# A two-layer graph attention network: W1's product by Strassen's half products, and x brought back in layer 2 by an identity product

## The chip, the core and the metric

The kernel runs on one core of one Trainium2 chip, in one launch. Each number called a time is the device time of one execution in microseconds. TensorE is called PE, VectorE DVE, ScalarE ACT, GpSimd POOL and SyncE SP, as the profile calls them.

## The reference

There are N = 10000 nodes with 768 numbers each and 170000 edges, sorted by destination, self loops among them; the network adds one more self loop per node. The reference computes

```python
h  = gat(x, W1, a_src1, a_dst1, b1)          # 768 -> 4 heads x 256
h1 = relu(layer_norm(h, g1, be1)) + x @ Wr1 + br1
h  = gat(h1, W2, a_src2, a_dst2, b2)         # 1024 -> 1 head x 768
h2 = layer_norm(h, g2, be2) + h1 @ Wr2 + br2
out = layer_norm(x + h2)                     # all in fp32
```

where `gat` multiplies by W, takes a softmax over the edges of each destination of `leaky_relu(alpha_src[src] + alpha_dst[dst])`, and sums the sources' rows with these weights.

## The kernel before

The nodes are handled in 79 tiles of 128 (NT = 79). The kernel has three parts, one after the other, and in each the order of instructions is written out by hand: an engine takes its instructions in the order in which the Python code issues them, and there is no planner.

**The projection** makes `x @ W1` for one tile after the other. `product` (its matmul is L172) issues six contraction steps for each of two halves of 512 columns into one PSUM tile of two banks called `big`. An fp32 matmul shows as two records in the trace. ACT copies the product to `row` (L667). DVE multiplies the product, read from PSUM, by `ad_b` and `as_b` (L670), and ACT sums each head's 256 elements (L673): these are the nodes' parts of the logits. POOL adds `b1` to `row` (L675), and SP stores the row to `table1`. After each tile one step is taken from a list of steps, which consists of two generators that run side by side:

- `prepare` sorts the edges into slots: for 80 columns it counts how many entries of `most` (128x1408) lie below an id, three counts a step, all on DVE (L240 into `less`, then the cast L242 to `at`, gathers of edge chunks by POOL at L245, and the remainder L231, L233). Later come the prefix sums over degrees (L277 adds into `before`), ranks, 79 scatters on POOL (L314), and the windows of sources that become `slots`.
- `weight_steps` multiplies W2 with the attention vectors (L645, L646), and computes two products with br1, the bias of the first residual, since the residual is kept without it: `after2`, which is `be2 + br2 + br1 @ Wr2` made in eight pieces (L653, added at L654), and `shift` and `lift`, which are `br1 @ W2`.

**Layer 1** gathers neighbours. POOL issues one indirect DMA for each slot (L425: 128 rows of 1033 floats from `table1`) into a ring of slots in SBUF, in the order of tiles; a gather waits until the slot's old row has been read. Nodes are sorted by degree into tiles, and the tiles' slots rise and then fall over the layer, 1377 in all; the ring holds 29 of them in layer 1 and 41 in layer 2. For a tile the logits (L478) need all its rows. The weighted sum is split: a few slots on PE as products with diagonal matrices, which ACT makes from `ident` (`summed`: L735 makes a `[P, H1, P]` buffer per slot, of which there are three, and L739 multiplies), the others on DVE (L520, or L516 after ACT's L509). `from_x` transposes the tile's gathered rows of x on PE for the residual product with Wr1 (L709), then POOL adds `after2` to the same rows (L717) and SP stores them to `x_d`. `L573` to `L589` are the layer norm (statistics, Ln and Exp on ACT, scaling), `L809` adds the residual, and L826 multiplies the result with W2.

**Layer 2** gathers rows of `table2` in the same way. Per tile PE makes the residual `h1 @ Wr2` (`residual`, L946, into `big`), and into free columns of the same PSUM tile the last 256 columns of the weighted sum (L934, with diagonals by ACT at L933, and a bias product L929); DVE sums the first 512 columns (L520). `norms` finishes a tile: statistics L573, then `scaled` (L587, L589) with g2 as factor and, in place of be2, the row `x + after2` that layer 1 stored, so that x, br2 and br1's part come in as the first norm's bias. Then

```python
nc.vector.scalar_tensor_tensor(h, r[:, :C2], 1.0, h, op0=OP.mult, op1=OP.add, accum_out=total)   # L957
```

adds the residual and sums it, and six small and two wide ACT instructions (L961 to L966, with a Square over 768 elements at L962 for the variance) make the last norm. `fetch_x` loads h1 and `x_d` for the tile after next by SP, `x_d` into one of three buffers (`xs`).

Of the kernel before, what the change touches and what calls it, by code (L numbers as in the profile page):

```python
# [28 lines left out]
F32 = mybir.dt.float32  # L29
# [6 lines left out]
P = 128  # L36
# [43 lines left out]
def gnn_kernel(ctx, tc, x, x_cols, src, dst, src_col, dst_col, W1, a_src1, a_dst1, b1, g1, be1, Wr1, br1,  # L80
# [57 lines left out]
    after2 = consts.tile([P, C2], F32, name="after2")  # L138
# [52 lines left out]
    def prepare():  # L191

        with tc.tile_pool(name="prep", bufs=1, side="right") as pool, \
                tc.tile_pool(name="prep2", bufs=2, side="right") as pool2:
            rows = pool.tile([P, NA, P], I32, name="rows")
            nc.sync.dma_start(rows, bass.AP(tensor=dst.tensor, offset=0, ap=[[P, P], [P * P, NA], [1, P]]))
            nxt = pool.tile([P, NA, P], I32, name="nxt")
# [7 lines left out]
            fall = pool2.tile([P, NA * P], F32, name="less", bufs=1).rearrange("p (a e) -> p a e", e=P)  # L205
# [9 lines left out]
            for a in range(NA):  # L215
# [6 lines left out]
                           allow_small_or_imprecise_dtypes=True)  # L222
            whole = pool.tile([P, NB], F32, name="whole")
# [12 lines left out]
            for j in range(0, NB, STEP):  # L236
                m = min(STEP, NB - j)
                for i in range(j, j + m):
                    less = pool2.tile([P, NA * P], F32, name="less", bufs=1)
                    nc.vector.tensor_scalar(less, most.rearrange("p a e -> p (a e)"), ids[:, i:i + 1], 0.0,  # L240
                                            op0=OP.is_lt, op1=OP.add, accum_out=whole[:, i:i + 1])
                nc.vector.tensor_copy(at[:, j:j + m], whole[:, j:j + m])  # L242
                chunk = pool2.tile([P, STEP, P], I32, name="chunk")
                for i in range(m):
                    nc.gpsimd.indirect_dma_start(  # L245
                        out=chunk[:, i, :], out_offset=None, in_=dst.rearrange("(c e) o -> c (e o)", e=P),
                        in_offset=bass.IndirectOffsetOnAxis(ap=at[:, j + i:j + i + 1], axis=0))
                for r in asked:
                    remainder(*r)
                asked = [(j, m, chunk)]  # L250
                yield
# [22 lines left out]
            before = pool.tile([P, NT + 1, D], BF16, name="before")  # L274
# [12 lines left out]
            facts = pool.tile([P, NT, 4], I32, name="facts")  # L287
# [11 lines left out]
            while s < D:  # L299
                more = pool.tile([P, D], F32, name=f"more{s}")  # L300
                nc.vector.tensor_add(more[:, :D - s], base[:, :D - s], base[:, s:])
                nc.vector.tensor_copy(more[:, D - s:], base[:, D - s:])
                base, s = more, 2 * s
# [38 lines left out]
            others = [pool.tile([P, NT, 4], I32, name=n) for n in ("rows", "nxt", "info")]  # L342
# [260 lines left out]
    with tc.tile_pool(name="w1", bufs=1) as w1p, tc.tile_pool(name="l1", bufs=2) as io, \  # L603
            psum_for_products(), tc.manual_schedule():
# [23 lines left out]
        def weight_steps():  # L628

            with nc.allow_non_contiguous_dma(reason="1024 numbers"):
                nc.scalar.dma_start(br1_c, br1.rearrange("(k p) -> p k", p=P))
            yield
            yield
            brT = spread_br1(w1p, "brT")
            load(w2, W2)
            nc.sync.dma_start(after2, bass.AP(tensor=be2.tensor, offset=be2.offset, ap=[[0, P], [1, C2]]))
            part = spread(w1p, br2, "part", nc.sync)
            for i, a in enumerate((a_dst2, a_src2)):  # L640
                vec = spread(w1p, a, "a2")
                for k in range(K1):
                    yield
                    m = io.tile([P, C1], F32, name="scr")[:, :C2]
                    nc.vector.tensor_mul(m, w2[:, k, :C2], vec)  # L645
                    nc.scalar.activation(m, m, AF.Copy, accum_out=w2[:, k, C2 + i:C2 + i + 1])  # L646
            load(wr1, Wr1)
            nc.vector.tensor_add(after2, after2, part)
            for k in range(K1):
                part = w1p.tile([P, C2], F32, name="part")  # L650
                nc.sync.dma_start(part, Wr2[k * P:(k + 1) * P, :])
                yield
                q = product(brT[:, k:k + 1, :], part[:, None, :], C2)  # L653
                nc.vector.tensor_add(after2, after2, q[:, :C2])  # L654
            yield
            q = product(brT, w2, R2)
            row = io.tile([P, R1], F32, name="row")
            nc.scalar.copy(row[:, :R2], q[:, :R2])
            nc.vector.tensor_add(lift, row[:, C2:C2 + 1], row[:, C2 + 1:R2])
            nc.scalar.dma_start(shift, row[0:1, :C2])  # L660
# [3 lines left out]
        for t in range(NT):  # L664
            p = product(xTs.pop(t), w1, C1)
            row = io.tile([P, R1], F32, name="row")
            nc.scalar.copy(row[:, :C1], p[:, :C1])  # L667
            for i, vec in enumerate((ad_b, as_b)):
                m = io.tile([P, C1], F32, name="scr")
                nc.vector.tensor_mul(m, p[:, :C1], vec)  # L670
                for h in range(H1):
                    s = slice(h * DH1, (h + 1) * DH1)
                    nc.scalar.activation(m[:, s], m[:, s], AF.Copy,  # L673
                                         accum_out=row[:, C1 + i * H1 + h:C1 + i * H1 + h + 1])
            nc.gpsimd.tensor_add(row[:, :C1], row[:, :C1], b1_b)  # L675
            load_x(t + 2)
            nc.sync.dma_start(table1[t * P:(t + 1) * P, :R1 - 1], row[:, :R1 - 1])
            next(steps, None)
# [9 lines left out]
    def ordered_layer1():  # L688
        nc.scalar.add_instruction(mybir.InstLoadActFuncSet(name=nc.get_next_instruction_name(), act_func_set_id=6, engine=nc.scalar.engine))
        with tc.tile_pool(name="b1", bufs=1) as pool, tc.tile_pool(name="small1", bufs=2) as small, \  # L690
# [22 lines left out]
            def from_x(t):  # L713

                xT = pool.tile([P, K0, P], F32, name="xT")
                moves = halves(xT, xt)
                nc.gpsimd.tensor_add(xt, xt, after2)  # L717
                nc.sync.dma_start(x_d[t], xt)
                return xT, moves
# [10 lines left out]
            def summed(acc, e, q, lo, hi, m):  # L730

                for k in range(lo, hi):
                    diagonals = pool.tile([P, H1, P], F32, name="diagonals", bufs=3)
                    for i in range(H1):
                        nc.scalar.activation(diagonals[:, i, :], ident, AF.Copy, scale=e[:, k, i:i + 1])  # L735
                    for i in range(H1):

                        c, d = i * DH1, (i + 1) * DH1
                        nc.tensor.matmul(acc[:, c:d], diagonals[:, i, :], ring.slot(q + k)[:, c:d],  # L739
# [4 lines left out]
            def weights_of(t):  # L744
# [5 lines left out]
                acc = ps_acc.tile([P, 2 * BANK], F32, name="acc")  # L750
                for lo, hi in ((0, min(m, 2)), (min(m, 2), m)):
                    summed(acc, e, FIRST[t], lo, hi, m)
                    yield acc
# [23 lines left out]
            for t in range(NT + 1):  # L777
# [66 lines left out]
                if live and not whole:  # L844
# [5 lines left out]
                    def some(q, e):  # L850
                        m = min(ON_PE1, e.shape[1])
                        summed(sums, e, q, 0, m, m)
                        return sums, m
# [22 lines left out]
    def ordered_layer2():  # L876
        nonlocal ps_big
        with tc.tile_pool(name="b2", bufs=1) as pool, tc.tile_pool(name="small2", bufs=2) as small, \
# [15 lines left out]
            firsts = [at_end(C1) for _ in range(min(2, NT))][::-1]  # L894
            xs = [parts[2][:, :D0], parts[3][:, :D0], after2]

            def fetch_x(t):

                hT = firsts[t] if t < 2 else parts[t % 2]
                nc.sync.dma_start(hT, h1_d[t])  # L900
                nc.sync.dma_start(xs[t % 3], x_d[t])
                return hT.rearrange("p (k n) -> p k n", n=P)
# [3 lines left out]
            added = spread(pool, shift, "out", nc.sync)  # L906
            b2_b = spread(pool, b2, "b2", nc.sync)
            ins[1] = fetch_x(1)
            g2_b = spread(pool, g2, "g2", nc.sync)
            nc.vector.tensor_add(b2_b, b2_b, added[:, :C2])  # L910
# [27 lines left out]
            def residual(t):  # L938


                hT = ins.pop(t)
                r = ps_big.tile([P, 2 * BANK], F32, name="big")
                for c in range(0, C2, BANK):
                    d = min(C2, c + BANK)
                    for j in range(K1):
                        nc.tensor.matmul(r[:, c:d], hT[:, j, :], wr2[:, j, c:d], start=(j == 0),  # L946
# [4 lines left out]
            def norms(t, h, r, means):  # L951
# [3 lines left out]
                scaled(h, means, stats, g2_b, xs[t % 3])  # L955
                total = small.tile([P, 1], F32, name="all")
                nc.vector.scalar_tensor_tensor(h, r[:, :C2], 1.0, h, op0=OP.mult, op1=OP.add, accum_out=total)  # L957
                yield
                o = pool.tile([P, C2], F32, name="out")
                less = small.tile([P, 1], F32, name="less")  # L960
                nc.scalar.activation(less, total, AF.Copy, scale=-1.0 / C2)  # L961
                nc.scalar.activation(o, h, AF.Square, bias=less, accum_out=total)  # L962
                nc.scalar.activation(total, total, AF.Ln, bias=eps, scale=1.0 / C2)
                nc.scalar.activation(total, total, AF.Exp, scale=-0.5)
                nc.scalar.activation(less, less, AF.Copy, scale=total)
                nc.scalar.activation(o, h, AF.Identity, bias=less, scale=total)  # L966
# [5 lines left out]
            assert C2 % BANK and C2 % BANK + C2 - ON_PE2 <= BANK  # L972
            rs = {0: residual(0)}
# [3 lines left out]
            for t in range(NT):  # L977
# [11 lines left out]
                else:  # L989
# [21 lines left out]
                    for _ in last:  # L1011
                        pass
                    last = norms(t, h, rs[t], [acc, rs[t][:, C2:2 * C2 - ON_PE2]])
# [274 lines left out]
```

## The time and the profile before

| | |
|---|---|
| runs | 5824.71, 5810.66, 5822.92 us |
| median | 5822.92 us |
| profiled execution | 5824.71 us, span 5822.9 us, mean granted PE clock 0.907 |
| busy share of the span | PE 84%, DVE 72%, POOL 57%, ACT 50% |
| DMA | mean 274 GB/s, 1594 MB moved, 1287 MB of it by POOL's queue |
| stages (read from the first and last instructions of each) | projection to 935 us, layer 1 to 3705 us, layer 2 to the end |

The busy share is a mean over three stages that have different limits, so each stage is read by itself. "Idle before" in a group of instructions is the time in which the engine stood still just ahead of them, with the instruction that ended most of that. A number behind an x is a count of instructions.

### The profile page before, as it was taken

Reading aid. Unit: us, or ns where it says so; the run is one execution under the profiler, and the core shown is the slowest. Engines: PE = TensorE matmul, PEld = TensorE weight load, DVE = VectorE, ACT = ScalarE, POOL = GpSimd, SP = SyncE. Lnnn points to the kernel's source line nnn. Section 1 sums busy time; section 2 is a strip of 40 time slices with the busy share of each in tenths; the row PEclk is TensorE's granted clock in tenths of the full one; section 3 lists DMA queues with packets and bytes.
Section 4 is the critical chain, followed back from the end, with each engine's and each line's share of the span. In section 5 each row is a group of like instructions: output and inputs, shape, how many; then the busy total and the mean of one; then the engine's idle time right before and its main releaser. Section 6 shows DMA issues by size and latency. Waiting matters only on the chain. (4 is left out here: it accounts for less than half of the span.)

```text
span 5822.9 us, 58833 instructions
## 1 busy us (share of the span) xinstructions
PE 4867.7 (84%) x14875; PEld 2883.8 (50%) x14875; DVE 4202.1 (72%) x7498; ACT 2927.9 (50%) x8500; POOL 3346.5 (57%) x3238
## 2 busy tenths in 40 slices
PE   9899996999988766568888999798888756778898
PEld 3344443555555444344555555455555534455565
DVE  5765244998877776778778899587766756767787
ACT  3333443777766665667766777343333323333333
POOL 3435465666555655655556665366666656666664
PEclk9999998999999888788999999899888877888899
DMA  4323636898888875778888898699998878889896
GB/s 156 122 93 84 89 93 228 312 344 333 306 309 317 323 291 215 286 294 306 317 316 334 335 341 302 245 334 329 328 314 301 311 255 291 305 309 318 313 339 216
DMA packets 475455, 1594.46 MB, mean 274 GB/s; under 512 B 118456, under 2 KB 122616, under 8 KB 475111
## 3 DMA queue, kind: packets, MB, share of 16 engines
q0 software_dynamic: 322384, 1286.62, 60.9%
q1 hardware_dynamic: 150672, 300.58, 15.5%
q10 hardware_dynamic: 2054, 3.42, 0.2%
q8 instruction: 125, 2.05, 0.1%
q14 instruction: 220, 1.79, 0.1%
HBM read 1434.95 MB, written 177.29 MB: 277 GB/s over the span
## 5 line engine op out<-in xcount | busy, mean ns | idle before, releaser
L425 POOL DMA_INDIRECT ring<-table,slots x2675 | 2619.6, 979 | 1353.4 <-issue 664.0
L520 DVE SCALAR_TENSOR_TENSOR acc<-ring,e,acc 128x512 f32<-128x512 f32 (+1 forms) x2530 | 1582.1, 625 | 219.2 <-PE acc L739 117.7
L509 ACT ACTIVATE ring<-ring,e 128x256 f32<-128x256 f32 x3284 | 1339.1, 506 | 12.9 <-issue 12.2
L516 DVE TENSOR_TENSOR acc<-acc,ring 128x1024 f32<-128x1024 f32 x801 | 985.6, 1230 | 82.0 <-issue 6.7
L934 PE MATMUL big<-ring,diagonals 128*128 128x256 f32 x2754 | 762.1, 433 | 274.9 <-issue 202.5
L946 PE MATMUL big<-wr,w 128*128 128x512 f32 (+1 forms) x2464 | 862.9, 503 | 110.9 <-issue 109.4
L172 PE MATMUL big<-w,xT 128*128 128x512 f32 x1896 | 834.4, 601 | 41.1 <-issue 18.5
L739 PE MATMUL acc<-ring,diagonals 128*128 128x256 f32 x1912 | 536.8, 441 | 376.4 <-ACT diagonals L735 203.8
L172 PE MATMUL big<-wr,xT 128*128 128x512 f32 x1896 | 835.2, 597 | 0.2 <-issue 0.2
L826 PE MATMUL half<-w,hT 128*128 128x512 f32 (+1 forms) x2528 | 830.4, 486 | 0.0
L934 PEld LDWEIGHTS big<-ring,diagonals 128*128 128x128 f32 x2754 | 594.0, 219 | 444.8 <-issue 281.9
L946 PEld LDWEIGHTS big<-wr,w 128*128 128x128 f32 x2464 | 483.4, 197 | 473.8 <-issue 441.1
L933 ACT ACTIVATE diagonals<-ident,e 128x128 f32<-128x128 f32 x1377 | 422.5, 388 | 550.6 <-remote 256.5
L739 PEld LDWEIGHTS acc<-ring,diagonals 128*128 128x128 f32 x1912 | 425.3, 225 | 479.7 <-ACT diagonals L735 220.7
L826 PEld LDWEIGHTS half<-w,hT 128*128 128x128 f32 x2528 | 477.8, 189 | 372.8 <-issue 327.4
L172 PEld LDWEIGHTS big<-w,xT 128*128 128x128 f32 x1896 | 364.2, 193 | 503.3 <-issue 485.4
L172 PEld LDWEIGHTS big<-wr,xT 128*128 128x128 f32 x1896 | 357.2, 192 | 421.6 <-issue 421.6
L486 ACT ACTIVATE e<-e 128x68 f32<-128x68 f32 (+29 forms) x160 | 38.2, 239 | 968.8 <-DVE e L485 386.9
L717 POOL TENSOR_TENSOR xt<-xt,after 128x768 f32<-128x768 f32 x79 | 146.3, 1852 | 492.3 <-PE half L709 492.3
L735 ACT ACTIVATE diagonals<-ident,e 128x128 f32<-128x128 f32 x956 | 294.2, 387 | 224.5 <-DVE e L500 93.7
L670 DVE TENSOR_TENSOR scr<-big,ad_b 128x1024 f32<-128x1024 f32 x79 | 96.7, 1224 | 420.1 <-ACT row L667 396.3
L675 POOL TENSOR_TENSOR row<-row,none 128x1024 f32<-128x1024 f32 x79 | 186.9, 2366 | 306.8 <-ACT row L667 305.8
(174 smaller groups left out, 3548.7 us busy)
## 6 DMA issues: line engine op xcount, KB each, us to landing
ring<-table,slots POOLq DMA_INDIRECT x2675
table<-row SPq DMA_DIRECT2D x79, 516.0 KB
h_d<-hT SPq DMA_DIRECT2D x79, 512.0 KB
w<-h_d SPq DMA_DIRECT2D x77, 512.0 KB
table<-row SPq DMA_DIRECT2D x79, 385.0 KB
ring<-table SPq DMA_DIRECT2D x79, 385.0 KB
xT<-in_x_cols_dram SPq DMA_DIRECT2D x79, 384.0 KB
x_d<-xt SPq DMA_DIRECT2D x79, 384.0 KB
```

The costliest lines, as they stand in the source:

```text
L172: nc.tensor.matmul(p[:, c:e], aT[:, j, :], w[:, j, c:e], start=(j == 0), stop=(j == k - 1))
L425: nc.gpsimd.indirect_dma_start(out=to, out_offset=None, in_=table, in_offset=bass.IndirectOffsetOnAxis(ap=index, axis=0), **more)
L509: nc.scalar.activation(row[:, s], row[:, s], AF.Copy, scale=e[:, h:h + 1])
L516: nc.vector.tensor_add(acc[:, :c], acc[:, :c], row[:, :c])
L520: nc.vector.scalar_tensor_tensor(acc[:, s], row[:, s], e[:, h:h + 1], (acc if first is None else first)[:, s], op0=OP.mult, op1=OP.add)
L675: nc.gpsimd.tensor_add(row[:, :C1], row[:, :C1], b1_b)
L735: nc.scalar.activation(diagonals[:, i, :], ident, AF.Copy, scale=e[:, k, i:i + 1])
L739: nc.tensor.matmul(acc[:, c:d], diagonals[:, i, :], ring.slot(q + k)[:, c:d], start=(k == 0 and c % BANK == 0), stop=(k == m - 1 and (d % ...
L826: nc.tensor.matmul(q, hT[:, j, :], w2[:, j, c:c + q.shape[1]], start=(j == 0), stop=(j == K1 - 1))
L933: nc.scalar.activation(diagonals[:, k % G, :], ident, AF.Copy, scale=e[:, k, :])
L934: nc.tensor.matmul(to, diagonals[:, k % G, :], ring.slot(FIRST[t] + k)[:, ON_PE2:C2], start=False, stop=(k == n - 1), skip_group_check=True)
L946: nc.tensor.matmul(r[:, c:d], hT[:, j, :], wr2[:, j, c:d], start=(j == 0), stop=(j == K1 - 1 and (d < C2 or not whole(t))), skip_group_che ...
```

## The change

Five things change.

1. The projection takes tile 0 alone and the other 78 in 39 pairs. For a pair the product is a 2x2 block product (two tiles by two halves of the contraction; two halves of the contraction by two halves of the columns), and it is made from seven half products in place of eight. Each has three contraction steps of 512 columns in its own PSUM bank (`ps_m`, six banks). Five sums of W1's blocks are made once (`bsums`, and `b12` and `b21` in place), five sums of x's blocks per pair (`pair`, one pair ahead), and seven additions put the results together in SBUF. Four `row` buffers take the place of two. The multiplications by `ad_b` and `as_b` read `row` in SBUF, not PSUM.
2. Every other count (even columns) is made on ACT as a sum of signs with a small correction; `less` becomes bf16 with two buffers. Some buffers of the preparation share memory under new names.
3. `after2` is gone: layer 1 stores x without an addition, and layer 2 adds x to the residual in PSUM by an identity product (512 and 256 columns); be2 is the first norm's bias, and `be2 + br2 + br1 @ Wr2` is put together at the start of layer 2 with one product of 32 records.
4. The last norm takes its statistics by DVE (`deviation` over two pieces of 384), in place of ACT's Square and its sums; ACT keeps Ln, Exp and the last scaling. x is fetched into two buffers, not three.
5. In layer 1 all diagonals of a tile lie in one buffer of `ON_PE1 * H1` matrices, and ACT makes those of a group of slots before PE's products are issued.

The core of the diff:

```diff
-                    less = pool2.tile([P, NA * P], F32, name="less", bufs=1)
-                    nc.vector.tensor_scalar(less, most..., ids[:, i:i + 1], 0.0,
-                                            op0=OP.is_lt, op1=OP.add, accum_out=whole[:, i:i + 1])
+                    less = pool2.tile([P, NA * P], BF16, name="less")
+                    if i % 2:
+                        nc.vector.tensor_scalar(less, most..., ids[:, i:i + 1], 0.0,
+                                                op0=OP.is_lt, op1=OP.add, accum_out=whole[:, i:i + 1])
+                        continue
+                    nc.scalar.activation(less, most..., AF.Sign, scale=-1.0,
+                                         bias=halves[:, i:i + 1], accum_out=whole[:, i:i + 1])
+                    nc.scalar.activation(whole[:, i:i + 1], whole[:, i:i + 1], AF.Copy, bias=0.5 * NA * P, scale=0.5)
...
-            for k in range(K1):
-                part = w1p.tile([P, C2], F32, name="part")
-                nc.sync.dma_start(part, Wr2[k * P:(k + 1) * P, :])
-                yield
-                q = product(brT[:, k:k + 1, :], part[:, None, :], C2)
-                nc.vector.tensor_add(after2, after2, q[:, :C2])
...
-        for t in range(NT):
-            p = product(xTs.pop(t), w1, C1)
-            row = io.tile([P, R1], F32, name="row")
-            nc.scalar.copy(row[:, :C1], p[:, :C1])
+        def finish(t, row):
             for i, vec in enumerate((ad_b, as_b)):
                 m = io.tile([P, C1], F32, name="scr")
-                nc.vector.tensor_mul(m, p[:, :C1], vec)
+                nc.vector.tensor_mul(m, row[:, :C1], vec)
...
+        def pair(t):
+            a1, a2 = (xTs.pop(i) for i in (t, t + 1))
+            a11, a12, a21, a22 = (a[:, k, :] for a in (a1, a2) for k in (upper, lower))
+            sums = io.tile([P, 5, KH, P], F32, name="sums")
+            for i, (a, op, b) in enumerate(((a11, OP.add, a12), (a21, OP.add, a22), (a11, OP.add, a22),
+                                            (a21, OP.subtract, a11), (a12, OP.subtract, a22))):
+                nc.vector.tensor_tensor(sums[:, i], a, b, op=op)
+            return a11, a22, sums
...
+        for t in range(1, NT, 2):
+            a11, a22, sums = ready
+            r1, r2 = new_row(), new_row()
+            m3 = times(a11, b12)
             load_x(t + 2)
+            m5 = times(sums[:, 0], b22)
+            nc.scalar.copy(r1[:, right], m5)
+            load_x(t + 3)
+            m2 = times(sums[:, 1], b11)
+            nc.scalar.copy(r2[:, left], m2)
+            nc.vector.tensor_sub(r2[:, right], m3, r2[:, left])
+            m4 = times(a22, b21)
+            nc.vector.tensor_sub(r1[:, left], m4, r1[:, right])
+            nc.vector.tensor_add(r1[:, right], r1[:, right], m3)
+            nc.vector.tensor_add(r2[:, left], r2[:, left], m4)
+            if t + 2 < NT:
+                ready = pair(t + 2)
+            m1 = times(sums[:, 2], bsums[:, 0])
+            nc.vector.tensor_add(r2[:, right], r2[:, right], m1)
+            m6 = times(sums[:, 3], bsums[:, 1])
+            nc.vector.tensor_add(r2[:, right], r2[:, right], m6)
+            times(sums[:, 4], bsums[:, 2], m1)
+            nc.vector.tensor_add(r1[:, left], r1[:, left], m1)
+            finish(t, r1)
+            next(steps, None)
+            finish(t + 1, r2)
             next(steps, None)
...
-                nc.gpsimd.tensor_add(xt, xt, after2)
                 nc.sync.dma_start(x_d[t], xt)
...
-                    diagonals = pool.tile([P, H1, P], F32, name="diagonals", bufs=3)
...
+                diagonals = pool.tile([P, ON_PE1 * H1, P], F32, name="diagonals")
...
+                    nc.tensor.matmul(r[:, c:d], ident, xt[:, c:d], start=True, stop=False,
+                                     skip_group_check=True)
                     for j in range(K1):
-                        nc.tensor.matmul(r[:, c:d], hT[:, j, :], wr2[:, j, c:d], start=(j == 0),
+                        nc.tensor.matmul(r[:, c:d], hT[:, j, :], wr2[:, j, c:d], start=False,
...
-                scaled(h, means, stats, g2_b, xs[t % 3])
-                total = small.tile([P, 1], F32, name="all")
-                nc.vector.scalar_tensor_tensor(h, r[:, :C2], 1.0, h, op0=OP.mult, op1=OP.add, accum_out=total)
+                scaled(h, means, stats, g2_b, be2_b)
+                nc.vector.tensor_add(h, h, r[:, :C2])
+                mean, inv = deviation(small, pieces(h, C2 // 2))
                 yield
+                less = small.tile([P, 1], F32, name="less")
+                nc.vector.scalar_tensor_tensor(less, mean, -1.0, inv, op0=OP.mult, op1=OP.mult)
...
-                nc.scalar.activation(less, total, AF.Copy, scale=-1.0 / C2)
-                nc.scalar.activation(o, h, AF.Square, bias=less, accum_out=total)
-                nc.scalar.activation(total, total, AF.Ln, bias=eps, scale=1.0 / C2)
-                nc.scalar.activation(total, total, AF.Exp, scale=-0.5)
-                nc.scalar.activation(less, less, AF.Copy, scale=total)
-                nc.scalar.activation(o, h, AF.Identity, bias=less, scale=total)
+                nc.scalar.activation(o, h, AF.Identity, bias=less, scale=inv)
```

## The prediction

> **What bounds the kernel now.** I read the page first, then the three stages as stretches, then in each stage the groups of instructions, the waits and a piece of the timeline. The columns of the stretches are length, then busy time and count of PE, its weight loads, DVE, ACT and POOL, then granted clock, DMA share and GB/s.
>
> ```profile
> PE 4867.7 (84%) x14875; PEld 2883.8 (50%) x14875; DVE 4202.1 (72%) x7498; ACT 2927.9 (50%) x8500; POOL 3346.5 (57%) x3238
> 0.00:935.00 935.00, 863.02 (x1993) 380.49 (x1993) 489.95 (x988) 356.85 (x1378) 421.74 (x326) 0.98 0.39 104
> 935.00:3705.00 2770.00, 2311.95 (x7442) 1385.25 (x7442) 2223.02 (x3599) 1867.34 (x4956) 1595.87 (x1535) 0.92 0.82 306
> 3705.00:5823.00 2118.00, 1692.67 (x5440) 1118.08 (x5440) 1489.14 (x2911) 703.71 (x2167) 1328.94 (x1377) 0.87 0.87 306
> ```
>
> The projection (to 935 us) is PE's: 863 of 935 us busy, DMA 0.39. In the other two DMA comes nearest to a bound (0.82, 0.87) with PE and DVE close behind, so there the gaps between transfers decide. A stretch of the projection without preparation on DVE, 600 to 641 us (groups):
>
> ```profile
> L172 PE MATMUL big<-w,xT 128*128 128x512 f32 x97 | 41.8, 592 | 0.0
> L673 ACT ACTIVATE scr<-scr 128x256 f32<-128x256 f32 x32 | 12.8, 402 | 5.2 <-DVE scr L670 5.2
> L670 DVE TENSOR_TENSOR scr<-big,ad_b 128x1024 f32<-128x1024 f32 x4 | 4.9, 1224 | 31.8 <-ACT row L667 23.8 <-issue 7.9
> ```
>
> PE never idles: four tiles of 24 records, 0.43 us from start to start, 10.3 us a tile; DVE is idle three quarters of the time. Where the preparation counts (80 to 330 us, 20 steps) that is otherwise:
>
> ```profile
> L240 DVE TENSOR_SCALAR_CACHE_REDUCE less<-most,ids 128x1408 f32<-128x1408 f32 x60 | 100.6, 1676 | 1.4
> L645 DVE TENSOR_TENSOR scr<-w,a 128x768 f32<-128x768 f32 x15 | 14.2, 949 | 0.0
> L231 DVE TENSOR_TENSOR below<-chunk,ids 128x384 f32<-128x384 int32 x19 | 10.6, 558 | 0.0
> ```
>
> Three counts a step cost 3 x (1.68 + 0.08) = 5.3 us of DVE, and a tile takes 11.4 us, 9.7 of them DVE's.
>
> Layer 1, one tile on POOL's timeline (idle time before an instruction and its releaser in brackets):
>
> ```profile
> 2139.92 1.81 POOL L717 TENSOR_TENSOR xt<-xt,after 128x768 f32<-128x768 f32 x1 [5.54 <-PE half L709]
> 2141.88 0.99 POOL L425 DMA_INDIRECT ring<-table,slots  x1 [0.15 <-issue]
> ...
> 2167.78 0.99 POOL L425 DMA_INDIRECT ring<-table,slots  x1 [0.30 <-issue]
> ...
> 2181.42 0.99 POOL L425 DMA_INDIRECT ring<-table,slots  x1 [0.30 <-issue]
> 2188.09 1.81 POOL L717 TENSOR_TENSOR xt<-xt,after 128x768 f32<-128x768 f32 x1 [5.67 <-PE half L709]
> 2190.05 0.99 POOL L425 DMA_INDIRECT ring<-table,slots  x1 [0.15 <-issue]
> ```
>
> Gathers go out 1.30 us apart until the ring is full; the next burst stands behind the add L717, which waits for PE's transposes of the same tile. In those waits the DMA share is 0.48. The waits of the layer put sizes on it:
>
> ```profile
> POOL xt L717 <- PE half L709: 492.3, 78, 18.4
> DVE e L478 <- DMA ring<-table,slots: 153.4, 33, 25.1
> ```
>
> The first is the add's; the second is what it costs, DVE's logits waiting for the tile's last gather. Layer 2's groups:
>
> ```profile
> L946 PE MATMUL big<-wr,w 128*128 128x512 f32 x1232 | 561.0, 606 | 26.0 <-issue 25.9
> L957 DVE SCALAR_TENSOR_TENSOR w<-big,w 128x768 f32<-128x768 f32 x79 | 75.6, 957 | 3.0 <-DVE w L589 0.3
> L573 DVE BATCH_NORM_STATS2 st<-big 128x6 f32<-128x256 f32 x79 | 33.7, 427 | 277.8 <-remote 130.3 <-PE big L946 81.4 <-PE big L934 48.8
> ```
>
> DVE idles 278 us ahead of L573, much of it for PE; the residual L946 is PE's largest fixed piece.
>
> **Projection.** A pair of tiles had 48 records; seven half products of six records make 42, so 42 x 0.43 = 18.0 us in place of 20.6: 2.57 a pair, 100 us over 39 pairs if PE stays the bound. DVE gets more. Per pair: five sums of 128x384 at 0.56 (by L231, 2.8), seven adds of 128x512 (0.69 by layer 1's statistics L573, 4.8), four multiplications at 1.22 (4.9): 12.5 us where 4.9 were. The seventh product accumulates into the first one's bank, so PE waits there for DVE to read that bank, and DVE then waits for PE: a hole of some 1.5 us a pair, six records less what DVE does meanwhile. In quiet steps 12.5 + 1.5 hides under 18.0.
>
> In a pair of count steps: 12.5, three counts still on DVE (5.3), two remainders with their sums (2.2), L645 twice (1.9), two casts (0.3) are 22.2 us. The other counts go to ACT (L673 takes 0.40 for 256 elements and L667 1.01 for 1024, so some 1.4 for 1408, and 0.19 for its read), behind eight accumulations. The cast L242 on DVE waits for them, and behind it stand the remainder, the next multiplications and adds: some 4 us in the step with two ACT counts, 0.5 in the other. With the hole, 28.2. Tiles 4 to 18 took 22.8 a pair: 7.5 x 5.4 = +41. Tiles 19 to 30 took 29.8 a pair, because the eight Wr2 products wait for DMA there; those leave this stage, so 26.3: 6 x 3.5 = -21. The steps of the prefix adds L277 have 37 us of DVE in 55 us: 37 + 2.5 x 14 = 72, +17. The rank steps -5. Steps 40 to 49 are POOL's, six scatters of 1.27 and the add of 2.37 are 10.0 a tile: 0. Steps 50 to 77 keep DVE's window work and fall from 20.6 to about 19.5 a pair: 14 x 1.1 = -15. The five sums of W1 (128x1536, some 9 us) delay the start by 6. Sum +23, say **+25**. Bounds: -95 if PE carries everywhere, +90 if DVE also loses 1.7 us in every pair to order.
>
> One more thing is in the trace: DVE reading two SBUF tensors and a POOL add reading SBUF don't run side by side.
>
> ```profile
> 993.62 1.28 DVE L589 SCALAR_TENSOR_TENSOR h<-h,sd,be 128x1024 f32<-128x1024 f32 x1
> 993.87 2.71 POOL L717 TENSOR_TENSOR xt<-xt,after 128x768 f32<-128x768 f32 x1 [1.47 <-PE half L709]
> ```
>
> Here the add took 2.71 in place of 1.81 us, the 0.9 that was left of L589 and a little. The multiplications now read `row` from SBUF (before: PSUM), so POOL's b1 add may stretch by up to 1.2 to 2.4 beside the partner tile's; it costs only in the five POOL-bound pairs, up to 12 us, inside the bounds.
>
> The Trainium skill ("SBUF — State Buffer", Who interferes with whom) says that a DVE instruction with two SBUF inputs contends with a GpSimd one that reads SBUF, and that on the pair of ports they share the first holds it for its whole instruction. The row agrees for a DVE that started first; none here shows the other order. If DVE were always the blocked one, an estimate by that rule is 2.37 for each of 78 adds, up to 185 us of DVE, and the projection would end at the upper bound or past it.
>
> **Layer 1.** Removed: L717, 146 us of POOL, and its wait of 492. The x_d store on SP no longer waits for POOL, but h1_d's behind it still waits for ACT. What the first gather of a burst waits for now is the slot's last reader, PE L739. In the tile shown L739 starts at 2178.4; the first slot's eight records at the half clock of that stretch (0.43 apart) end about 2182, so that gather can go at 2182.4 in place of 2190.05. The next ones come no faster than L739 frees slots: some 6 us are won. DVE can use at most what L478 waits: 153.4 less the first tile's 25.1 is 128, and 22 more put down to issue, 150. The 28 tiles of at most 15 slots run at 25 us with PE idle 0.5: nothing there. I take **-120**; bounds -150 and -20, the latter if slots come free no earlier. The diagonals in one buffer of 16, not three of four, take away waits of about 1 us (ACT on PE) of ACT, off the path: 0.
>
> **Layer 2.** Added to PE: two identity products a tile, 512 and 256 wide, 2 x (0.43 + 0.216) = 1.29 us, 102 us in all. In the 28 tiles of at most 15 slots PE is the bound (16 to 19 us, idle 0 to 3): 28 x 1.29 = 36. In the 43 of 16 to 22 slots DMA is 0.91 to 1.00 busy and PE's own stalls follow transfers; I take half, 28. The eight larger ones follow DMA: 0. The product of br2's part, once in eight pieces before, now stands ahead of the first residual: 32 records, 10.3 us, covered by 7.7 us in which PE waits for the first x_d and h1_d, and 7.7 before the first L934: 0, or 10 without that cover. DVE: L957 (1.04 with its read) becomes an add (0.95), two statistics of 384 (0.55 each, between L573's 0.42 for 256 and 0.69 for 512), an aggregate (0.24) and a small product (0.07), +1.3 a tile; ACT loses 1.6 a tile. DVE's 629 us without work in this stage hide it; without that cover it would be 103. SP fetches x into two buffers, not three, and behind a wait for PE in place of DVE, half a tile early: 0. Sum 64, say **+65**, bounds 0 and +130.
>
> **Sum.** 25 - 120 + 65 = -30. The profiled execution took 5824.7 (span 5822.9 and 1.8 around it), against a median of 5822.9: 5794.7, say 5795.
>
> **Rivals.** Slower: layer 1's turn stays. The gathers wait in POOL's order for PE L739 of a tile whose logits waited for the last gather; if releases are put on later readers, or the x gather (now behind the x_d store) holds the queue, the add's place is taken by a wait as long. Then -20 in place of -120: 5895. It speaks for it that L717 and L739 hang on the same PE stream; against it that the transposes come after L739's 32 records. It decides when the first gather of a burst starts less than 2 us earlier than now. Faster, PE stays the projection's bound: -95, so 25 + 95 = 120 lower, 5675; the quiet steps speak for it, the 9.7 of 11.4 us of DVE in count steps against. Faster, layer 2's products vanish behind DMA: +10, so 5740; 0.87 DMA share speaks for it, the small tiles against.
>
> **How the numbers follow.** A measurement here tells 0.3%, 17.5 us, from no change: 5805 and 5840. The forecast has 0.42, with its own range 5755 to 5850; of it 0.23 lies under 5805, 0.12 between, 0.07 above. The slower rival 0.36 (0.35 above, 0.01 between), PE-bound 0.10, hidden products 0.12, both faster. Faster 0.45, same 0.13, slower 0.42. The range 5690 to 5915 leaves out most of PE-bound and the tail of the slower rival with unfavourable terms elsewhere.
>
> **What would show it.** Right: projection some 960 us long, DVE waiting at the cast in count steps; in layer 1 no L717, L478's waits near 30 us, DMA share 0.85; layer 2 some 65 us longer with DVE's wait ahead of the first statistics grown. Wrong: a projection of 840 us with PE at 0.95 or more, or ring gathers in layer 1 with some 450 us of waits for PE.

## The result and the profile after

The changed kernel took 5956.4 us in the median (5951.8 to 5965.9), the kernel before 5816.8 beside it: a ratio of 1.0244, 95% interval 1.022 to 1.0268, so about 2.4% slower where 0.5% faster was forecast. The profiled execution took 5965.9 us, 5964.0 of it span.

Each stage runs from the end of the one before; layer 1 begins with its first gather (of x), layer 2 when SP has issued layer 1's last store. The page's first line, and then the three stages of the changed kernel as stretches (length, then busy time and count of PE, its weight loads, DVE, ACT and POOL, granted clock, DMA share, GB/s):

```profile
PE 4884.3 (82%) x14957; PEld 2881.9 (48%) x14957; DVE 4559.6 (76%) x8123; ACT 2838.2 (48%) x8306; POOL 3265.3 (55%) x3159
```

```profile
0.00:1206.00 1206.00, 821.68 (x1727) 351.42 (x1727) 752.04 (x1373) 384.62 (x1500) 458.85 (x326) 0.85 0.28 78
1206.00:3780.00 2574.00, 2256.77 (x7442) 1348.86 (x7442) 2220.90 (x3599) 1858.53 (x4955) 1474.93 (x1456) 0.95 0.91 329
3780.00:5964.00 2184.00, 1805.84 (x5788) 1181.63 (x5788) 1586.64 (x3151) 595.05 (x1851) 1331.57 (x1377) 0.88 0.85 297
```

| stage | before | after | difference | forecast |
|---|---|---|---|---|
| projection | 938.0 | 1206.1 | +268 | +25 |
| layer 1 | 2765.7 | 2572.0 | -194 | -120 |
| layer 2 | 2119.2 | 2185.9 | +67 | +65 |
| span | 5822.9 | 5964.0 | +141 | -30 |

In the projection no engine is full: PE 822 and DVE 752 of 1206 us, DMA 0.28. So its length is set by a loop of waits. Those of 40 to 1160 us name its links (engine, line that waited, what it waited for, us in total, times, longest):

```profile
PE m L692 <- DVE row L738: 317.8, 34, 21.4
DVE row L742 <- PE m L692: 138.4, 36, 4.8
DVE sums L716 <- DMA xT<-in_x_cols_dram: 94.7, 31, 14.0
DVE at L248 <- ACT whole L247: 62.3, 27, 4.0
DVE row L730 <- ACT row L729: 45.6, 18, 3.2
```

In the changed kernel's numbering L692 are the half products, L738 reads the first product's bank, L742 adds it again once the seventh product has been accumulated there, L716 are the sums of x's blocks, L618 loads x, L677 are the multiplications by `ad_b` and `as_b`, L682 is POOL's addition of b1, and L729 is one of ACT's two copies. One turn of the loop on the timeline, in a step with little preparation:

```profile
818.62 2.35 POOL L682 TENSOR_TENSOR row<-row,none 128x1024 f32<-128x1024 f32 x1 [14.63 <-DVE scr L677]
819.09 2.97 DVE L677 TENSOR_TENSOR scr<-row,ad_b 128x1024 f32<-128x1024 f32 x1 [0.70 <-ACT scr L680]
821.98 1.21 DVE L677 TENSOR_TENSOR scr<-row,as_b 128x1024 f32<-128x1024 f32 x1
...
826.37 0.69 DVE L730 TENSOR_TENSOR row<-m,row 128x512 f32<-128x512 f32 x1 [3.18 <-ACT row L729]
...
827.78 0.39 SPq L351 DMA_DIRECT2D hot<-order_d  x1
828.26 6.90 SPq L618 DMA_DIRECT2D xT<-in_x_cols_dram  x2
...
837.81 0.56 DVE L716 TENSOR_TENSOR sums<-xT 128x384 f32<-128x384 f32 x1 [8.83 <-DMA xT<-in_x_cols_dram]
838.75 1.97 DVE L716 TENSOR_TENSOR sums<-xT 128x384 f32<-128x384 f32 x4 [0.38 <-DMA xT<-in_x_cols_dram]
840.64 0.68 DVE L738 TENSOR_TENSOR row<-row,m 128x512 f32<-128x512 f32 x1
841.37 4.67 PE L692 MATMUL m<-bsums,sums 128*128 128x512 f32 x6 [10.65 <-DVE row L738]
...
845.88 2.74 PE L692 MATMUL m<-w,xT 128*128 128x512 f32 x6
846.08 0.69 DVE L742 TENSOR_TENSOR row<-row,m 128x512 f32<-128x512 f32 x1 [3.97 <-PE m L692]
```

The loads of x go out only at 828.3, since SP takes them after the second tile's store, which waits for POOL and ACT. DVE stands 8.8 us at the sums, and the read L738 is queued behind them; for that read PE's seventh product waits 10.7 us. It then takes 4.67 us for six records that take 2.74 in the next product, and DVE waits for it in turn. This pair took 30.8 us where its products need 18.0.

Part of that wait for x is particular to this turn and the next. The loads stand directly behind a load of the preparation (L351), are issued over 6.9 us in place of 1.2, and land 9.5 us after the first was asked for; in the turn before, without L351 ahead of them, x landed after 4.4 us, DVE waited 1.6, and the pair took 21.7. Of the 39 pairs eight wait 7 us or more for x, six of them scatter or quiet pairs. In the count steps only one waits at all (4.4 us), in the window steps none longer than 0.3.

### The profile page after: what moved, and what is told of

Same layout as the page of the kernel before. It is cut to its first block, busy times and chain, and to the rows that moved or that the text cites. A ratio compares the mean times of both kernels' runs of the same rounds, so it can differ in the third digit from the quotient of the medians.

```text
span 5964.0 us, 59720 instructions
## 1 busy us (share of the span) xinstructions
PE 4884.3 (82%) x14957; PEld 2881.9 (48%) x14957; DVE 4559.6 (76%) x8123; ACT 2838.2 (48%) x8306; POOL 3265.3 (55%) x3159
## 3 DMA queue, kind: packets, MB, share of 16 engines
q14 instruction: 226, 1.85, 0.1%
## 5 line engine op out<-in xcount | busy, mean ns | idle before, releaser
L431 POOL DMA_INDIRECT ring<-table,slots x2675 | 2649.8, 991 | 1731.7 <-issue 521.5
L526 DVE SCALAR_TENSOR_TENSOR acc<-ring,e,acc 128x512 f32<-128x512 f32 (+1 forms) x2530 | 1578.3, 624 | 150.6 <-PE acc L807 48.9
L1020 PE MATMUL big<-wr,w 128*128 128x512 f32 (+1 forms) x2464 | 890.9, 506 | 163.1 <-issue 161.6
L1006 PE MATMUL big<-ring,diagonals 128*128 128x256 f32 x2754 | 743.1, 429 | 171.3 <-issue 137.4
L807 PE MATMUL acc<-ring,diagonals 128*128 128x256 f32 x1912 | 481.9, 410 | 232.4 <-ACT diagonals L801 170.8
L692 PE MATMUL m<-bsums,sums 128*128 128x512 f32 x702 | 383.4, 700 | 326.3 <-DVE row L738 326.3
L680 ACT ACTIVATE scr<-scr 128x256 f32<-128x256 f32 x632 | 253.5, 402 | 735.7 <-DVE scr L677 720.5
L807 PEld LDWEIGHTS acc<-ring,diagonals 128*128 128x128 f32 x1912 | 388.8, 206 | 318.2 <-ACT diagonals L801 187.9
L682 POOL TENSOR_TENSOR row<-row,none 128x1024 f32<-128x1024 f32 x79 | 188.6, 2388 | 618.4 <-DVE scr L677 356.9
L692 PEld LDWEIGHTS m<-bsums,sums 128*128 128x128 f32 x702 | 153.6, 225 | 541.4 <-DVE row L738 358.2
L583 ACT ACTIVATE sd<-mv,eps 128x1 f32<-128x1 f32 x237 | 69.4, 293 | 693.0 <-DVE mv L581 409.3
```

Of the source, the lines that this page charges most:

```text
L431: nc.gpsimd.indirect_dma_start(out=to, out_offset=None, in_=table, in_offset=bass.IndirectOffsetOnAxis(ap=index, axis=0), **more)
L526: nc.vector.scalar_tensor_tensor(acc[:, s], row[:, s], e[:, h:h + 1], (acc if first is None else first)[:, s], op0=OP.mult, op1=OP.add)
L692: nc.tensor.matmul(to, a[:, k, :], b[:, k, :], start=(p is None and k == 0), stop=(k == a.shape[1] - 1), skip_group_check=True)
L807: nc.tensor.matmul(acc[:, c:d], diagonals[:, k * H1 + i, :], ring.slot(q + k)[:, c:d], start=(k == 0 and c % BANK == 0), stop=(k == m - 1 ...
L1006: nc.tensor.matmul(to, diagonals[:, k % G, :], ring.slot(FIRST[t] + k)[:, ON_PE2:C2], start=False, stop=(k == n - 1), skip_group_check=True)
```

## The experiments

Runs without an interval are one execution each and are compared by their stages, since chips differ: on the chip of the first four runs the kernel before takes 5505 us, and the variants of the changed kernel spend some 1897 us in layer 2 there in place of some 2180. Layer 1 agrees between the chips within 25 us, the projection within 7.

**Loads a pair earlier.**

```diff
-                xTs[t] = io.tile([P, K0, P], F32, name="xT", bufs=3)
+                xTs[t] = io.tile([P, K0, P], F32, name="xT", bufs=4)
-            load_x(t + 2)      # behind m3; load_x(t + 3) behind m5
+            load_x(t + 4)      # behind m3; load_x(t + 5) behind m4
```

> The changed kernel with four xT buffers, not three, and each pair's loads of x asked for a pair earlier (tiles t+4 and t+5), ahead of the stores of the pair before last in SP's order. Theory L (load): in the changed kernel a pair takes 28 to 31 us because the loads stand in SP's order behind both stores of the pair before, land some 9.5 us after they are issued, and the five sums that read them stand in DVE's order ahead of the read of the first product's bank, for which PE's seventh product waits (318 us in all). Then the pair falls to about 22 us, the projection from 1206 to 920 to 990 us, the run from 5956 to 5680 to 5750. Theory W (work): DVE's sheer work and ACT's counts set the pair; then the projection stays within 30 us of 1206.

The projection took 1109.0 us: 97 less, not the 220 to 290 expected. The theory holds for two kinds of pairs and fails for two: the three quiet pairs fell from 21.7, 30.8 and 30.8 us to 19.6 each and pairs of scatter steps from 30 to 23.9, but pairs of the first count steps (31 to 32) and of the window steps (some 28.2) did not move, as they had hardly waited for x. There the loop has other links, and the waits show them:

```profile
PE m L693 <- DVE row L740: 239.3, 35, 21.4
DVE row L744 <- PE m L693: 134.5, 38, 4.8
```

These are the first product's bank again (numbers shifted by one or two lines): PE waits for DVE's read, DVE for the product that follows.

**Sums later in DVE's order.**

```diff
-            if t + 2 < NT:
-                ready = pair(t + 2)
             m1 = times(sums[:, 2], bsums[:, 0])
...
             finish(t + 1, r2)
+            if t + 2 < NT:
+                ready = pair(t + 2)
```

> The changed kernel with three xT buffers and its loads where they were, but the five sums of the next pair issued on DVE after the second tile of the pair is finished, not ahead of the read of the first product's bank. Theory L: PE's seventh product no longer waits for a load, which gets the rest of the pair to land; quiet pairs fall to 19 to 22 us and the projection to 900 to 980. Rival: the load itself is the loop (stores, loads, sums, products, stores), then the sums wait in their new place as long and the projection stays above 1150. Theory W: within 30 us of 1206.

1184.1 us, 22 less: the rival's number, not the theory's 900 to 980. Whether for the rival's reason, that the load is the loop, the next run tells.

> Both edits: early loads and late sums. Theory L: no wait of DVE for x is left; what sets a pair then is the chain seventh product, its addition, four multiplications, ACT's accumulations, the two copies, the additions, the seventh product, some 19 to 20 us against 18.0 of PE; the projection is 860 to 940, at most 20 us under the better of the two single edits. Theory W: within 30 us of 1206.

1182.9 us: the early loads now bring nothing, so it isn't the load that holds this order. With the sums late, PE waits for them at the second product of the next pair (110 us) and for banks that are read late:

```profile
PE m L693 <- ACT scr L681: 160.6, 20, 20.2
PE m L693 <- DVE sums L718: 110.1, 13, 9.5
```

The wait was moved from PE's seventh product to its second, with PE's other five products behind it. Theory L covers only the quiet and scatter pairs; it was replaced by G, a loop whose links are all of DVE's order, PE's seventh product and ACT's copies.

**Without POOL's addition of b1** (with both edits above):

> As with early loads and late sums, and POOL's addition of b1 to the rows of the projection is left out. In the changed kernel the first multiplication of the second tile takes 2.97 us beside that addition, where it takes 1.22 alone. If that blocking is on the chain, 1.75 us a pair, up to 68 us, go from the projection against the run with both edits; if the pair is PE's by then, 10 us or less.

1140.3 us, 43 less: the addition is on the chain in this order. Most of what it stretches here are the sums (150.5 us of DVE with the addition, 94.5 without) and not multiplications as in the row of 2.97 us above (the first of each tile: 112.1 with it, 96.6 without). That the stores go out earlier without the addition is not separated from this. In the changed kernel itself nine multiplications are stretched by 1.74 us each, 16 us in all, and the sums take 98.7 us, some 4 more than without the addition; so the 43 us do not carry over to it.

**The two kernels again, on one chip.**

> The kernel before, once more, with a profile: the experiments so far ran on a chip where it takes 5505 us, not 5823, and the stages have to be compared on one chip. All theories: projection 938 and layer 1 2766 us within 30; what is shorter on this chip should be layer 2 (about 1830 in place of 2119), since the variants of the changed kernel had 1897 there in place of 2186.

> The changed kernel on the same chip as the kernel before. Projection 1206 and layer 1 2560 us within 20, layer 2 about 1900, some 65 more than the kernel before has on this chip if that difference does not depend on the chip.

Before 939.0, 2743.4 and 2116.8; after 1212.8, 2563.4 and 2175.0. This chip was another one again, on which the kernel before takes 5803 us, so layer 2's 1830 was not seen; the stage differences, +274, -180 and +58, repeat those of the first pair of profiles.

**Without the identity products.**

> The changed kernel without the two identity products a tile in layer 2 (x is not added). If PE's 1.29 us a tile are the cost of the new layer 2, about 65 us of its length go against the changed kernel on this chip; if the price is in the norm moved to DVE or in the start of the layer, less than 20.

Layer 2 took 2131.0 us, 44 less: between the two expectations, nearer to the first. Three quarters of layer 2's +58 are PE's identity products, without which PE is busy 99 us less; the other 14 are the norm on DVE and the start of the layer together, which no run separates.

**Layer 1 without POOL's addition**, in the kernel before:

```diff
-                nc.gpsimd.tensor_add(xt, xt, after2)
```

> The kernel before without POOL's addition of after2 to x in layer 1, all else as before (the bias row lacks that term). If the addition's place in POOL's order is the cause of layer 1's 196 us, layer 1 falls from 2766 to 2560 to 2600 us; if the one buffer of diagonals has a share in it, layer 1 stops above 2650.

Layer 1 took 2568.7 us, 175 less than on the same chip before, and within 6 us of the changed kernel. The addition explains 175 of the 180 us; for the single buffer of diagonals at most 5 are left.

**The seventh product in its own bank** (with early loads):

```diff
-            times(sums[:, 4], bsums[:, 2], m1)
-            nc.vector.tensor_add(r1[:, left], r1[:, left], m1)
+            m7 = times(sums[:, 4], bsums[:, 2])
+            nc.vector.tensor_add(r1[:, left], r1[:, left], m1)
+            nc.vector.tensor_add(r1[:, left], r1[:, left], m7)
```

> The changed kernel with early loads (as the first of these runs, projection 1109 us), and the seventh product goes to a PSUM bank of its own and is added by one more DVE instruction, in place of accumulating into the first product's bank. Theory G (loop through the shared bank): PE waited 239 us there for DVE's read of the first product, and DVE then 134 us for PE's seventh; both go, one addition of 0.69 a pair comes, the projection falls by 80 to 130 us to 980 to 1030. Theory W: DVE is the bound by its work, then 27 us are added.

1005.6 us, 103 less, as G said: pairs of count steps 28.1, of window steps 24.6, quiet ones 18.1, which is PE's 18.0. The largest wait of PE that is left is now for an ACT copy (L728), which stands behind ACT's accumulations:

```profile
PE m L693 <- ACT row L728: 127.8, 28, 12.6
```

**All counts on DVE** (with early loads, the shared bank):

> The changed kernel with early loads (projection 1109 us) and all counts on DVE. DVE gets 40 x 1.76 = 70 us more and loses its waits for ACT's counts, 62 us: within 20 us of 1109 if the count's place makes no difference; 1060 or less if ACT's counts are what stretches the count steps; 1160 or more if DVE's work there is the bound.

1109.5 against 1109.0 us: where the counts are made makes no difference in this loop. What ACT's counts save DVE in work, it loses waiting for them.

**Own bank, and ACT's copies ahead of the second tile's accumulations:**

```diff
             nc.scalar.copy(r2[:, left], m2)
+            if t > 1:
+                finish(t - 1, r2_before)
+                next(steps, None)
...
-            finish(t + 1, r2)
-            next(steps, None)
+            r2_before = r2
```

> As with early loads and the own bank, and the second tile of a pair is finished in the next pair, behind ACT's two copies of that pair's products, so that DVE does not wait for copies that stand behind sixteen accumulations (48 us in the run with early loads). Theory G: no wait of DVE for PE or ACT is left outside the count steps, the projection is 920 to 980 us. If 950 is not undercut, DVE's work (some 780 us) and its waits for ACT's counts and the windows remain and the scheme cannot beat 938.

982.3 us, just beyond the upper end of what was expected and 44 over the kernel before. Neither PE nor DVE is full: of 982 us PE is busy 790, DVE 786. PE's wait for L728 is gone, but one for the sums has come in its place, and DVE's wait for ACT's counts is still there:

```profile
PE m L693 <- DVE sums L718: 92.5, 16, 19.9
DVE at L248 <- ACT whole L247: 81.1, 27, 11.8
```

**Layer 1 with the addition moved, not removed.** In the kernel before, the addition and the store of x go to where the next x is gathered:

```diff
-                nc.gpsimd.tensor_add(xt, xt, after2)
-                nc.sync.dma_start(x_d[t], xt)
...
                 def next_x():
                     nonlocal xt
-                    xt = fetch_x(t + 1)
+                    keep_x(t)          # the two lines from above
+                    if t + 1 < NT:
+                        xt = fetch_x(t + 1)
```

> The kernel before with POOL's addition of after2 and the store of x moved in the order from ahead of the gathers to just ahead of the next tile's gather of x; nothing is left out. If the addition's place and not its 1.85 us is the cause of layer 1's difference, layer 1 falls by 150 to 180 us, the other stages stay, and the run is 0.968 to 0.975 of the kernel before; if the addition itself costs POOL time on the path, by less than 100.

A miss: the ratio is 1.02 (1.0184 to 1.0216), layer 1 2896.3 us. The turn was not removed but replaced:

```profile
2309.52 1.82 POOL L721 TENSOR_TENSOR xt<-xt,after 128x768 f32<-128x768 f32 x1
2317.71 0.98 POOL L425 DMA_INDIRECT xt<-in_x_dram,order  x1 [6.37 <-DMA x_d<-xt]
```

x has one buffer, so its gather waits until the store has read it, 510 us over the layer in POOL's waits, and the ring's gathers stand behind.

**The old projection under the changed layers.**

> The changed kernel with the projection and the counts of the kernel before (one tile at a time, eight half products, all counts on DVE), but without the eight Wr2 products there; layers 1 and 2 as changed. If the loss is the seven-product projection alone, this run has a projection of 915 to 938 us, layer 1 about 2565, layer 2 about 60 above the kernel before: 0.972 to 0.980 of the kernel before. If part of layer 1's gain came from the new projection, layer 1 is above 2650 and the ratio above 0.985.

Projection 888.9, layer 1 2565.0, layer 2 2204.6: 0.9663 of the kernel before (0.9643 to 0.9683). The projection is shorter than any forecast: leaving out the eight Wr2 products with their waits for DMA takes 50 us from it, where the prediction had 21. Measured from there the new projection costs 1206 - 889 = 317 us.

**The addition behind the first gathers, and x's gather seven slots later.**

```diff
+                    events.append((first + 2, lambda: keep_x(t)))
-                    events.append((first + 2, next_x))
+                    events.append((first + 9, next_x))
```

> The kernel before with POOL's addition and the store of x behind the first gathers of the burst, as in the run with the later addition, and the gather of the next x seven slots later again, so that the store has landed by then (it waited 482 us for it there). If only the order was the cause, layer 1 is 2570 to 2620, layer 2 as before, the run 0.965 to 0.975 of the kernel before. If the addition in the middle of a burst holds gathers back by its 1.85 us a tile, layer 1 is 2650 to 2720 and the run 0.98 to 0.99.

Layer 1 2565.7, layer 2 2134.5, projection 939.4 us: 0.963 of the kernel before (0.9614 to 0.9646), the lowest ratio here. Layer 1's gain needs neither the identity products nor a removal, only other places for the addition and for the gather of x. Layer 2, left as in the kernel before, takes 70 us less than the new one in the run above on the same chip, which agrees with its +58 and +67.

## Why the prediction was wrong

**Projection: wrong, and more than the whole miss.** +268 for +25, 243 too many, where the span missed by 171 because layer 1 gave some of it back. The step that failed is "In quiet steps 12.5 + 1.5 hides under 18.0", and with it "0" for the scatter steps and "about 19.5" for the window steps: each pair was costed as the larger of PE's work and DVE's, where it is a loop through both. Its parts:
- The loads of x had no term at all in the sum. 97 us (first run), most of it in the scatter and quiet pairs: they stand behind both stores in SP's order, and the sums that need them stand ahead of L738 in DVE's.
- The hole at the shared bank was sized at 1.5 us, and taken to be hidden. It was 3.8 on average (138 us over 36 pairs), and PE waited 318 us on its other side. With a bank of its own and the loads early, another 103 us went.
- ACT's copies behind sixteen accumulations had no term: 23 us (982.3 against 1005.6).
- The wait at the cast L248 was right: 4.0 us in the step with two counts on ACT, 0.6 in the other. A pair of count steps was forecast at 28.2 us, took 31 to 32, and takes 28.1 once loads and bank are put right; that this meets the forecast is in part luck, for the forecast holds a hole of 1.5 us that is gone with the bank.
- In the other direction, the Wr2 products that left the stage were worth 50 us, not 21.

The loads, the bank and the copies, 97, 103 and 23 us, make 223 of the 317 that the new projection costs against the old one without the Wr2 products. What is left, 982 against 889 us, goes with DVE's work: 786 us where it had 482, in a stage in which PE saves only 843 - 790 = 53 us of busy time. Both are busy four fifths of the time and the waits shown with that run remain. No run took that work away by itself, so this last part is read from the profile and its cause is not shown.

The clock adds to the hole. In the timeline above the six records of the seventh product took 4.67 us after PE had been idle for 10.65, and the next six 2.74; in the turn before, after 3.20 us of idle, they took 2.84. The stage's clock fell from 0.97 to 0.85. The Trainium skill ("TensorE: Matmul & The Clock Gate", HAM oscillation) says that an idle gap of more than some 3.4 us sends PE to half rate for the work that follows; the rows agree.

**The shared ports: right in kind.** The row that the prediction showed had POOL wait for DVE; the one above has DVE wait for POOL, 2.97 us in place of 1.22. So both orders occur, as the page cited there says ("SBUF — State Buffer", Who interferes with whom); the upper bound by that rule, 185 us, was far off, with 16 us in the changed kernel's multiplications and some 4 in its sums.

**Layer 1: mechanism right, size low.** -194 (-180 on the second chip) for -120, outside the bound of -150. The mis-sized term is the ceiling: it was DVE's wait for the last gather alone. That wait did not even vanish (153 to 74 us), but with gathers earlier other waits went too, DVE's for PE's part of the sum (117.7 to 48.9 us) among them, and PE's clock rose from 0.92 to 0.95. Which of these made the rest of the gain is read from the waits, not shown. The wait for PE's part before, and both waits after:

```profile
DVE acc L520 <- PE acc L739: 117.7, 57, 6.2
DVE e L484 <- DMA ring<-table,slots: 73.5, 19, 26.8
DVE acc L526 <- PE acc L807: 48.9, 43, 4.8
```

The slower rival, that the turn stays, is refuted for the change itself: the ring's gathers wait 135 us for PE there, not the 450 that stood as its sign. What it describes is what the run with the moved addition showed.

**Layer 2: right in its sum, in part by luck.** +67 and +58 for +65; of the 58, 44 are the identity products (64 forecast) and 14 the rest (0 forecast, with the cover of the other engines), so two errors of opposite sign nearly cancel. The added work is seen in the groups of the layer:

```profile
L579 DVE BATCH_NORM_STATS2 st<-w 128x6 f32<-128x384 f32 x158 | 80.6, 552 | 2.7
L1017 PE MATMUL big<-w,ident 128*128 128x512 f32 x154 | 80.3, 602 | 8.3 <-issue 6.8 <-DMA w<-x_d 1.5
```

**Signs.** The rival "PE stays the projection's bound" was furthest off. The result is slower, but not by the rival that stood for it.

## What to carry to other kernels

A step that runs through several engines in fixed orders costs the length of its loop, not the largest of its busy times: before costing a new product scheme, write down the order of one turn on each queue, the loads' queue too, and add up what each instruction stands behind. A product that accumulates into a bank that another engine reads in between ties the two engines together twice. And an instruction that waits in a queue that issues transfers costs what the transfers behind it lose, not its own time: here an addition of 1.85 us cost 2.2 us a tile where it stood and nothing that these runs tell behind the first gathers (layer 1 2565.7 us with it there, 2568.7 without it on another chip), and moving it together with the gather of x freed 3.7% of the run.

## What was not expected of the hardware

- Two chips differ by 300 us of 5800 in the kernel before; in the variants of the changed kernel nearly all of it is in layer 2, with projection and layer 1 within 25 us. A comparison needs both kernels on one chip.
- An instruction of DVE with two SBUF operands and an addition by POOL stretch each other in both orders: POOL 1.81 to 2.71 us behind DVE, DVE 1.22 to 2.97 behind POOL, and five sums together 2.43 to 5.06 us in the run with early loads:

```profile
729.54 5.06 DVE L718 TENSOR_TENSOR sums<-xT 128x384 f32<-128x384 f32 x5
729.93 2.36 POOL L683 TENSOR_TENSOR row<-row,none 128x1024 f32<-128x1024 f32 x1
```
